# Weight folding ahead of the first norm, with its copies on ScalarE, and small matrices built on GpSimd, in a four-layer attention and gate kernel

## Chip, cores and metric

The kernel runs on one core of a Trainium2 chip. The time is the device time of one execution in microseconds (us); lower is better. The chip's engines are named as in the profile: PE is TensorE (matmuls), PEld its weight loads, DVE is VectorE, ACT is ScalarE, POOL is GpSimd, SP is SyncE. DVE and ACT can read PSUM in this kernel; POOL is only given tiles in SBUF.

## What is computed

The input is x, 16 samples of 256 channels by 32 x 32 positions, float32. Four layers follow one another:

```python
# layer 0: group norm, one-head attention over the 1024 positions, projection, residual
xn = group_norm(x); q, k, v = W_qkv xn + b
out = W_proj (softmax(q^T k / sqrt(C)) v) + b_proj + x
# layer 1: a gate from the channel mean and maximum
w3 = relu(conv3x3(concat[mean, max], w1)); gate = sigmoid(conv3x3(mean + max + w3, w2)); x = x * gate
# layer 2: group norm, attention, projection, residual, as layer 0 with other weights
# layer 3: attention with 32 query channels, logits clipped to +-10, scaled by gamma, residual
```

## The kernel before

**Layout.** A sample is held as channels on partitions (`x`, two chunks of 128 channels by 1024 positions) and once more by tokens (`xr`). Matrix products of two by two blocks are done with seven block products and a number of additions (`seven`, `weighted`), which is why tiles such as `xs`, `mc`, `vc`, `tc`, `tv` hold sums or differences of blocks. Logits and their exponentials are tiles `e` of 128 x 8 x 512.

**Folding (`fold`, from L301).** For layers 0 and 2 the weights are folded once, at the start of the program, and used for all samples. `transposed(j)` turns the query, key and value weights (`raw` -> PSUM `wtp` -> `wt`) with four TensorE transposes each, and two copies out of PSUM at L316. `multiplied` forms m = Wq^T Wk / 16 and wvp = Wv^T Wp with eight matmuls each (L322), and copies each half out of PSUM at L329. `right_sums` (L283 on) makes the block differences, on DVE for m (tile `mc`) and on POOL for wvp (tile `vc`). Two folded biases follow: `tbp` -> `tb` (L344, L351) and `brp` -> `bcol` (L365, L372).

**The head (`head`, `group_norm`).** Before a sample can be worked on, its channels are normalised in place: per-channel statistics (L114, L117), a transposed exchange inside the group (L119 to L134), a power on POOL (L138), scale and offset (L141 to L144), and the two passes over the data: chunk 0 on DVE (L145), chunk 1 on ACT (L146), 1024 positions each in one instruction. The first matmul on data, `tb_l` at L571, reads m and the normalised sample 0.

**The order.** The code is written as Python generators that are stepped in turn, and the framework then orders each engine's queue when the program is built: earlier-traced work goes first, as far as it is expected to be ready. Each engine works through its queue strictly in order on the chip. `keep_in_program_order` holds an instruction behind the one traced before it on the same engine. Before the change, the first line that is stepped is `in_turn([head(0), fold("l0", ...)])`: one step of sample 0's norm, one step of the layer-0 fold, and so on. After that two streams of samples (even and odd) start, the second 30 steps behind the first, and beside them `later()` runs: `head(1)` in turn with the fold of layer 2, then `fold3` (the small matrices of layer 3: `w` scaled at L400, copied into `w3qk` on POOL at L410, then matmuls `bias` L417 and L426, `qb`/`bcol` L434 to L437, and `strips` L380), then `build_toep`, then `checks`.

**`build_toep` (L84).** Three 128 x 32 matrices for the 3x3 convolutions, each the sum of nine terms: 27 instructions at L95 (compare and multiply) and 24 additions at L98, then three copies at L101. They are first read by the gate's matmul (L169).

**`checks` (from L871).** Five small tests that the weights are fit for this path. Each begins with `whole` (L294): a 128 x 512 copy at L297 and a 128 x 128 subtraction at L298, whose result a DVE instruction squares or weighs (`sq` L796, `msq` L831); PE then sums it (`size` L801, `reach` L845), and the result is counted on POOL (`n_ok`).

Of the kernel before, what the change touches and what calls it, by code (L numbers as in the profile page):

```python
# [12 lines left out]
AF = mybir.ActivationFunctionType  # L13
ALU = mybir.AluOpType
AX = mybir.AxisListType

P = 128
C = 256
CC = C // P
HW = 1024  # L20
NT = HW // P
HALF = 512
NH = HW // HALF
# [15 lines left out]
L0_GAMMA, L0_BETA, L0_BQ, L0_BK, L0_BP = range(5)  # L39
# [17 lines left out]
class Const:  # L57
# [26 lines left out]
    def build_toep(self, tc, work, tidx):  # L84

        nc = tc.nc
        for k in range(3):
            for tap in range(9):
                w = self.sc[:, S_W1 + 9 * k + tap : S_W1 + 9 * k + tap + 1]
                if tap == 0:  # L90
                    one = self.toep[:, k, :]
                else:
                    one = work.tile([P, STRIP], FP, tag="tap", name=f"tap_{k}_{tap}")
                tc.keep_in_program_order(
                    nc.vector.tensor_scalar(one, tidx, float(tap), w, ALU.is_equal, ALU.mult)  # L95
                )
                if tap:
                    nc.vector.tensor_tensor(self.toep[:, k, :], self.toep[:, k, :], one, ALU.add)  # L98
            yield
        for g in range(1, NG):  # L100
            nc.vector.tensor_copy(self.toep[:, 2 + g], self.toep[:, 2])  # L101
        nc.vector.tensor_scalar(self.neg_b2, self.sc[:, S_B2 : S_B2 + 1], -1.0, None, ALU.mult)
        yield


def group_norm(nc, k, small, xt, out, gamma, beta, nm, keep=None):

    st = small.tile([P, CC, 2, 6], FP, tag="st", name=f"st_{nm}", bufs=2)  # L110
    mv = k.moments
    for c in range(CC):
        for h in range(NH):
            first = nc.vector.bn_stats(st[:, c, h, :], xt[:, c, h * TPH : (h + 1) * TPH])  # L114
            if keep is not None:
                keep(first)
        nc.vector.bn_aggr(mv[:, 2 * c : 2 * c + 2], st[:, c, :, :])  # L117
    row = small.tile([P, GROUP], FP, tag="row", name=f"row_{nm}", bufs=2)
    nc.vector.transpose(row, mv)  # L119
    yield  # L120
    rst = small.tile([P, 6], FP, tag="rst", name=f"rst_{nm}", bufs=2)
    nc.vector.bn_stats(rst, row)
    rmv = small.tile([P, 2], FP, tag="rmv", name=f"rmv_{nm}", bufs=2)
    nc.vector.bn_aggr(rmv, rst)
    wide = small.tile([P, 2, GROUP], FP, tag="wide", name=f"wide_{nm}", bufs=2)
    nc.vector.tensor_copy(wide, rmv.unsqueeze(2).to_broadcast([P, 2, GROUP]))
    both = small.tile([P, 2, GROUP], FP, tag="both", name=f"both_{nm}", bufs=2)
    nc.vector.transpose(
        both.rearrange("p i n -> p (i n)"), wide.rearrange("p i n -> p (i n)")
    )  # L130

    gm = both[:, 0, 0 : 2 * CC : 2]
    ve = small.tile([P, CC], FP, tag="ve", name=f"ve_{nm}")
    nc.vector.scalar_tensor_tensor(  # L134
        ve, both[:, 0, 1 : 2 * CC : 2], EPS, both[:, 1, 0 : 2 * CC : 2], ALU.add, ALU.add
    )
    rstd = small.tile([P, CC], FP, tag="rstd", name=f"rstd_{nm}")
    nc.gpsimd.tensor_tensor(rstd, ve, k.neg_half, ALU.pow)  # L138
    yield
    a = small.tile([P, CC], FP, tag="a", name=f"a_{nm}")  # L140
    nc.vector.tensor_tensor(a, rstd, k.vec[:, :, gamma], ALU.mult)  # L141
    bb = small.tile([P, CC], FP, tag="bb", name=f"bb_{nm}")
    nc.vector.tensor_tensor(bb, gm, a, ALU.mult)
    nc.vector.tensor_tensor(bb, k.vec[:, :, beta], bb, ALU.subtract)  # L144
    nc.vector.tensor_scalar(out[:, 0], xt[:, 0], a[:, 0:1], bb[:, 0:1], ALU.mult, ALU.add)  # L145
    nc.scalar.activation(  # L146
        out[:, 1], xt[:, 1], AF.Identity, bias=bb[:, 1:2], scale=a[:, 1:2]
    )
    yield


# [50 lines left out]
def fast_path(nc, tc, k, bad, x, w_l0, w_l2, w_l3, qk_bias, v_bias, tap_idx, out):  # L202
# [7 lines left out]
    with ExitStack() as ctx:  # L210
# [83 lines left out]
        def whole(w, nm):  # L294

            full = work.tile([P, CC, C], FP, tag="oc", name=f"full_{nm}", bufs=3)
            tc.keep_in_program_order(nc.vector.tensor_copy(full, w))  # L297
            nc.vector.tensor_tensor(full[:, 0, P:], w[:, 1, P:], w[:, 0, P:], ALU.subtract)  # L298
            return full

        def fold(nm, which, base):  # L301


            w = raw[nm]
            wt = expp.tile([P, 3, CC, C], FP, tag="e", name=f"wt_{nm}")

            def transposed(j):
                for o in range(CC):
                    ps = bank(f"wtp_{nm}_{j}_{o}")
                    for c in range(CC):  # L310
                        nc.tensor.transpose(
                            ps[:, c * P : (c + 1) * P],
                            w[:, c, j * C + o * P : j * C + (o + 1) * P],
                            k.ident,
                        )
                    nc.vector.tensor_copy(wt[:, j, o, :], ps[:, :C])  # L316

            def multiplied(dst, left, right, scale):
                for c in range(CC):
                    ps = bank(f"fold_{nm}_{c}")  # L320
                    for o in range(CC):
                        nc.tensor.matmul(  # L322
                            ps[:, :C],
                            left[:, o, c * P : (c + 1) * P],
                            right[:, o, :],
                            start=(o == 0),
                            stop=(o == CC - 1),
                        )
                    nc.vector.tensor_scalar(dst[:, c, :], ps[:, :C], scale, None, ALU.mult)  # L329

            transposed(0)
            yield
            transposed(1)
            yield

            m = wts.tile([P, CC, C], FP, name=f"m_{nm}")
            multiplied(m, wt[:, 0], wt[:, 1], C**-0.5)
            yield
            mc = right_sums(nc.vector, m, f"mc_{nm}")
            tb = wts.tile([P, CC], FP, name=f"tb_{nm}")  # L340
            ps = bank(f"tbp_{nm}")
            for c in range(CC):
                for o in range(CC):
                    nc.tensor.matmul(  # L344
                        ps[:, c : c + 1],
                        wt[:, 1, o, c * P : (c + 1) * P],
                        k.vec[:, o, base + 2 : base + 3],
                        start=(o == 0),
                        stop=(o == CC - 1),
                    )  # L350
            nc.vector.tensor_scalar(tb, ps[:, :CC], C**-0.5, None, ALU.mult)  # L351
            yield
            transposed(2)
            yield
            wvp = wts.tile([P, CC, C], FP, name=f"wvp_{nm}")
            wp = w[:, :, 3 * C : 4 * C]
            multiplied(wvp, wt[:, 2], wp, 1.0)
            yield
            vc = right_sums(nc.gpsimd, wvp, f"vc_{nm}")

            bcol = bcol0 if nm == "l0" else bcol2
            ps = bank(f"brp_{nm}")
            for c in range(CC):
                for o in range(CC):
                    nc.tensor.matmul(  # L365
                        ps[:, c : c + 1],
                        wp[:, o, c * P : (c + 1) * P],
                        vcol[:, which, o : o + 1],
                        start=(o == 0),
                        stop=(o == CC - 1),  # L370
                    )
            nc.vector.tensor_tensor(bcol, ps[:, :CC], k.vec[:, :, base + 4], ALU.add)  # L372
            folded[nm] = m, mc, wvp, vc, tb
            yield
# [555 lines left out]
        def attend(xt, y, weights, lane, nm, then):  # L930
# [39 lines left out]
                then(h, tt.rearrange("p h c n -> p h (c n)"))  # L970
            count(ri, nm)

        def head(b):

            fetch(b)
            xt = loaded.pop(b)
            by_chunk = xt.rearrange("p t c n -> p c t n")
            xr = tokens[b] = load_tokens(b)
            keep = tc.keep_in_program_order if b == 1 else None
            yield from group_norm(  # L980
                nc, k, small, by_chunk, by_chunk, L0_GAMMA, L0_GAMMA + 1, f"l0_{b}", keep
            )
            ready[b] = xt, xr

# [173 lines left out]
        def in_turn(gens):  # L1158

            gens = list(gens)  # L1160
            while gens:
                for g in list(gens):
                    if next(g, gens) is gens:
                        gens.remove(g)
                    else:
                        yield
# [17 lines left out]
                    yield  # L1184
            do_chores(first)

        for _ in in_turn([head(0), fold("l0", 0, L0_GAMMA)]):
            pass


# [10 lines left out]
        ps = bank("badp")  # L1201
# [317 lines left out]
```

## Time and profile before

| | us |
|---|---|
| time, median of 3 runs (lowest to highest) | 2702.78 (2701.82 to 2702.98) |
| span of the profiled execution (no separate time of it is given) | 2702.3 |
| PE busy in the span | 2658.2 (98%) |
| DVE busy | 2153.9 (80%) |
| ACT busy | 1327.9 (49%) |
| POOL busy | 45.4 (2%) |
| first matmul of any kind / first matmul on sample data (`tb_l`) | 4.53 / 23.40 |

The span is cut into the busy and idle time of each engine. A row of the timeline reads: start in us, duration in us, engine, line, operation, tile written <- tiles read, shape, how many were merged, and in brackets how long the engine sat idle before it and who ended the wait. Merged instructions overlap a little, so a row's duration is from the first start to the last end. A row of the windows gives, for a stretch of time, the busy time and instruction count of PE, PEld, DVE, ACT and POOL, then the granted TensorE clock (1.00 is full speed).

### The profile page before, as it was taken

The page shows a single profiled execution, that of the slowest core. Times are in us where ns is not written, and L with a number is a line of the kernel's source. Part 1 is how long each engine was busy: PE and PEld are TensorE (multiplying, and loading weights), DVE is VectorE, ACT ScalarE, POOL GpSimd, SP SyncE. Part 2 cuts the span into 40 slices and gives each one's busy share as a digit, 9 for nine tenths or more (in the row PEclk, how much of TensorE's full clock was granted, in tenths as well). Part 3 has the DMA queues.
Part 4 walks back from the last instruction along what each step waited for, and adds up shares of the span by engine and source line. Part 5 has one row for each costly group of instructions (what it writes and reads, how often), then busy time and mean ns, then how long its engine had stood idle before and what let it go on. Part 6 is the DMA issues. An engine that isn't in the chain of part 4 may idle for free.

```text
span 2702.3 us, 47717 instructions
## 1 busy us (share of the span) xinstructions
PE 2658.2 (98%) x18998; PEld 2366.0 (88%) x18998; DVE 2153.9 (80%) x4242; ACT 1327.9 (49%) x2810; POOL 45.4 (2%) x118
## 2 busy tenths in 40 slices
PE   8999999999999999999999999999999999999997
PEld 6888988888988889889889898988989889898897
DVE  7988886888778887788867888678887788868776
ACT  3454455544455445544455544554454544545443
POOL 1000000000000000000000000000000000000000
PEclk9999999999999999999999999999999999999999
DMA  4021111212111120211201212112111121101111
GB/s 115 1 63 48 56 32 24 63 48 63 25 46 50 42 76 9 55 48 48 63 16 48 63 35 61 32 32 63 48 48 32 32 63 55 40 17 34 52 34 41
DMA packets 134823, 123.07 MB, mean 46 GB/s; under 512 B 10689, under 2 KB 125633, under 8 KB 134593
## 3 DMA queue, kind: packets, MB, share of 16 engines
q1 hardware_dynamic: 132720, 118.63, 15.7%
q8 instruction: 152, 2.49, 0.4%
q10 hardware_dynamic: 1872, 1.31, 0.2%
q14 instruction: 79, 0.64, 0.1%
HBM read 69.58 MB, written 50.33 MB: 44 GB/s over the span
## 4 chain that ended last, share of the span: by engine, by line
PE 81%; DVE 13%; ACT 4%; issue 2%; DMA 1%; POOL 0%; DVEq 0%; SPq 0%; ACTq 0%
PE b_l L571 15%; PE c_l L571 11%; PE af_l L571 11%; PE sb_l L571 10%; PE sc_l L571 8%; PE sf_l L571 4%; PE sa_l L571 3%; PE vb_l L571 3%; PE tb_l L571 3%; PE vc_l L571 2%; PE tc_l L571 2%; PE s L1107 2%; DVE e_l L603 1%; DVE vt L603 1%; PE vf_l L571 1%
## 5 line engine op out<-in xcount | busy, mean ns | idle before, releaser
L672 ACT COPY e_l<-sb_l 128x512 f32<-128x512 f32 x384 | 222.5, 584 | 217.9 <-PE sb_l L571 216.7
L571 PE MATMUL sb_l<-t_l,x 128*128 128x256 f32 x1024 | 262.0, 386 | 0.3
L571 PE MATMUL b_l<-vt,e_l 128*128 128x128 f32 x2048 | 251.8, 275 | 0.0
L571 PEld LDWEIGHTS b_l<-vt,e_l 128*128 128x128 f32 x2048 | 244.2, 192 | 5.4 <-issue 2.3
L571 PEld LDWEIGHTS sb_l<-t_l,x 128*128 128x128 f32 x1024 | 180.5, 191 | 40.1 <-ACT e_l L672 11.2
L682 ACT ACTIVATE e_l<-e_l 128x512 f32<-128x512 f32 x256 | 160.9, 630 | 86.6 <-DVE e_l L603 85.7
L684 ACT ACTIVATE e_l<-e_l 128x1024 f32<-128x1024 f32 x128 | 135.5, 1059 | 118.4 <-DVE e_l L603 118.4
L571 PE MATMUL c_l<-tv,cb_l 128*128 128x129 f32 x1536 | 189.0, 275 | 0.2 <-DVE cb_l L698 0.2
L571 PEld LDWEIGHTS c_l<-tv,cb_l 128*128 128x128 f32 x1536 | 180.3, 191 | 6.9 <-PE qk L1072 3.1
L603 DVE TENSOR_TENSOR e_l<-sc_l,e_l 128x512 f32<-128x512 f32 x128 | 88.0, 687 | 116.6 <-PE sc_l L571 114.9
L925 ACT COPY vt<-vb_l 128x512 f32<-128x512 f32 x144 | 84.5, 587 | 147.2 <-PE vb_l L571 146.1
L487 ACT ACTIVATE xr<-xr,bstrip 128x128 f32<-128x128 f32 (+1 forms) x376 | 134.4, 443 | 44.1 <-DVE xr L494 44.1
L1123 ACT ACTIVATE e<-s 128x512 f32<-128x512 f32 x256 | 131.8, 606 | 22.1 <-PE s L1107 21.4
L756 ACT COPY acc_l<-c_l 128x256 f32<-128x256 f32 x96 | 35.4, 368 | 212.3 <-DVE ri_l L755 151.8
L571 PE MATMUL sc_l<-tc_l,xs_l 128*128 128x256 f32 x512 | 134.0, 384 | 2.3 <-DVE vt L603 2.3
L571 PE MATMUL af_l<-tv,e_l 128*128 128x128 f32 x1024 | 131.6, 278 | 4.3 <-ACT e_l L682 4.3
L571 PE MATMUL sc_l<-t_l,xs_l 128*128 128x256 f32 x512 | 133.0, 382 | 0.8
L571 PE MATMUL sa_l<-t_l,x 128*128 128x256 f32 x512 | 132.4, 381 | 0.0
L571 PE MATMUL sf_l<-tc_l,x 128*128 128x256 f32 x512 | 131.7, 380 | 0.0
L571 PE MATMUL sb_l<-tc_l,xs_l 128*128 128x256 f32 x512 | 131.7, 379 | 0.0
L571 PEld LDWEIGHTS af_l<-tv,e_l 128*128 128x128 f32 x1024 | 121.3, 192 | 10.8 <-ACT e_l L682 7.7
L1128 DVE TENSOR_SCALAR e<-e 128x1024 f32<-128x1024 f32 x128 | 83.0, 687 | 59.0 <-ACT e L1123 59.0
(245 smaller groups left out, 5984.6 us busy)
## 6 DMA issues: line engine op xcount, KB each, us to landing
x<-mid_x SPq DMA_DIRECT2D x64, 512.0 KB, 3.3
xr<-in_x_dram SPq DMA_DIRECT2D x64, 256.0 KB, 4.9
mid_x<-t_z SPq DMA_DIRECT2D x128, 128.0 KB, 2.3
mid_x<-t_l SPq DMA_DIRECT2D x128, 128.0 KB, 2.3
x<-in_x_dram SPq DMA_DIRECT2D x62, 256.0 KB, 4.0
out_dram<-xr SPq DMA_DIRECT2D x124, 128.0 KB, 2.3
raw_l<-in_w_l_dram SPq DMA_DIRECT2D x1, 1024.0 KB, 6.9
raw_l<-in_w_l_dram SPq DMA_DIRECT2D x2, 256.0 KB, 5.5
```

The lines of the kernel that those rows point to most:

```text
L487: nc.scalar.activation(y[:, s, ts], y[:, s, ts], AF.Identity, bias=bias[:, s : s + 1])
L571: mm = nc.tensor.matmul(out, left, right, start=fresh and m == 0 and (lone or i == 0), stop=(m == len(pairs) - 1), skip_group_check=True,)
L603: nc.vector.tensor_tensor(dst, src, dst, ALU.add)
L672: nc.scalar.copy(block(i, j), ps.rearrange("p (m n) -> p m n", m=2))
L682: nc.scalar.activation(part, part, AF.Exp)
L684: nc.scalar.activation(e[:, m : m + 2, :], e[:, m : m + 2, :], AF.Exp)
L756: nc.scalar.copy(acc[:, hi, c2], c[:, :, :P])
L925: nc.scalar.copy(block(i, j), ps.rearrange("p (m n) -> p m n", m=TPH))
L1107: nc.tensor.matmul(ss[g][:, j * 2 * P : (j + 1) * 2 * P].rearrange("p (t g j) -> p t g j", t=TPH, g=2), qk[gs, mh, 1 - blk, j * P : (j + 1 ...
L1123: nc.scalar.activation(by_strip[:, :, :, qa], ss[g].rearrange("p (m t n) -> p m t n", m=2, t=TPH), AF.Exp,)
L1128: nc.vector.tensor_scalar(part, part, EXP_MIN, EXP_MAX, ALU.max, ALU.min)
```

## The change

The copies of the folds out of PSUM (L316, L329, L351) move from DVE to ACT. The first norm is stepped once (loads, statistics, first exchange), then the whole layer-0 fold is traced, then the rest of the norm. In that norm alone both data passes are cut in two halves of 512 positions, and its ACT halves are held behind the last ACT copy of the fold's transposes. `build_toep` and `whole` move from DVE to POOL. `group_norm`'s later uses keep one part. Nothing is computed otherwise.

```diff
 build_toep:
-                    nc.vector.tensor_scalar(one, tidx, float(tap), w, ALU.is_equal, ALU.mult)
+                    nc.gpsimd.tensor_scalar(one, tidx, float(tap), w, ALU.is_equal, ALU.mult)
-                    nc.vector.tensor_tensor(self.toep[:, k, :], self.toep[:, k, :], one, ALU.add)
+                    nc.gpsimd.tensor_tensor(self.toep[:, k, :], self.toep[:, k, :], one, ALU.add)
-            nc.vector.tensor_copy(self.toep[:, 2 + g], self.toep[:, 2])
+            nc.gpsimd.tensor_copy(self.toep[:, 2 + g], self.toep[:, 2])
 group_norm(..., keep=None, parts=1, behind=None):
-    nc.vector.tensor_scalar(out[:, 0], xt[:, 0], a[:, 0:1], bb[:, 0:1], ALU.mult, ALU.add)
-    nc.scalar.activation(
-        out[:, 1], xt[:, 1], AF.Identity, bias=bb[:, 1:2], scale=a[:, 1:2]
-    )
+    for i in range(parts):
+        ts = slice(i * NT // parts, (i + 1) * NT // parts)
+        nc.vector.tensor_scalar(
+            out[:, 0, ts], xt[:, 0, ts], a[:, 0:1], bb[:, 0:1], ALU.mult, ALU.add
+        )
+        other = nc.scalar.activation(
+            out[:, 1, ts], xt[:, 1, ts], AF.Identity, bias=bb[:, 1:2], scale=a[:, 1:2]
+        )
+        if behind is not None:
+            behind(other)
 whole:
-            tc.keep_in_program_order(nc.vector.tensor_copy(full, w))
-            nc.vector.tensor_tensor(full[:, 0, P:], w[:, 1, P:], w[:, 0, P:], ALU.subtract)
+            tc.keep_in_program_order(nc.gpsimd.tensor_copy(full, w))
+            nc.gpsimd.tensor_tensor(full[:, 0, P:], w[:, 1, P:], w[:, 0, P:], ALU.subtract)
 fold:
-                    nc.vector.tensor_copy(wt[:, j, o, :], ps[:, :C])
+                    copied.append(nc.scalar.copy(wt[:, j, o, :], ps[:, :C]))
-                    nc.vector.tensor_scalar(dst[:, c, :], ps[:, :C], scale, None, ALU.mult)
+                    nc.scalar.activation(dst[:, c, :], ps[:, :C], AF.Copy, scale=scale)
-            nc.vector.tensor_scalar(tb, ps[:, :CC], C**-0.5, None, ALU.mult)
+            nc.scalar.activation(tb, ps[:, :CC], AF.Copy, scale=C**-0.5)
+        def behind_folds(ins):
+            tc.add_manual_dep(ins.ins, copied[-1].ins.name, <order only, no wait>)
 head(b): group_norm(...)
-                nc, k, small, by_chunk, by_chunk, L0_GAMMA, L0_GAMMA + 1, f"l0_{b}", keep
+                nc, k, small, by_chunk, by_chunk, L0_GAMMA, L0_GAMMA + 1, f"l0_{b}", keep,
+                1 if b else NH,
+                None if b else behind_folds,
-        for _ in in_turn([head(0), fold("l0", 0, L0_GAMMA)]):
+        first_head = head(0)
+        next(first_head)
+        for _ in fold("l0", 0, L0_GAMMA):
+            pass
+        for _ in first_head:
             pass
```

## The prediction, made before the changed kernel was run

> **What bounds the kernel now.** The page first, for who is busy:
>
> ```profile
> PE 2658.2 (98%) x18998; PEld 2366.0 (88%) x18998; DVE 2153.9 (80%) x4242; ACT 1327.9 (49%) x2810; POOL 45.4 (2%) x118
> PE 81%; DVE 13%; ACT 4%; issue 2%; DMA 1%; POOL 0%; DVEq 0%; SPq 0%; ACTq 0%
> ```
>
> PE bounds it. The change removes no matmul, so it can win only where PE idles (2702.3 - 2658.2 = 44.1 us in all) or runs below full speed. About 15.3 us of the idle time lie in the last 102 us (86.73 busy in the stretch 2600 to 2702), which this change doesn't touch. So I read PE's own waits, between 20 and 80 us, then the timeline of the start, then the clock by windows.
>
> ```profile
> PE strips_l L380 <- DVE bcol L437: 0.8, 1, 0.8
> PE bias L417 <- POOL w3qk L410: 0.7, 1, 0.7
> PE fold_l L322 <- DVE wt_l L316: 0.6, 2, 0.3
> PE c_l L571 <- DVE cb_l L698: 0.2, 1, 0.2
> ```
>
> That is all that PE waits in 60 us: 2.3 us. Before 20 us it is more:
>
> ```profile
> 4.53 1.94 PE L311 MATMUL wtp_l<-ident,raw_l 128*128 128x128 f32 x8 [4.53 <-DMA raw_l<-in_w_l_dram]
> 13.30 3.78 PE L322 MATMUL fold_l<-wt_l 128*128 128x256 f32 x8 [6.83 <-DVE wt_l L316]
> 16.88 1.71 PE L344 MATMUL tbp_l<-vec,wt_l 128*128 128x1 f32 x8
> 18.45 1.09 PE L311 MATMUL wtp_l<-ident,raw_l 128*128 128x128 f32 x4
> 19.78 2.97 PE L322 MATMUL fold_l<-raw_l,wt_l 128*128 128x256 f32 x8 [0.23 <-DVE wt_l L316]
> 22.59 0.95 PE L365 MATMUL brp_l<-vcol,raw_l 128*128 128x1 f32 x8
> 23.40 1.10 PE L571 MATMUL tb_l<-x,m_l 128*128 128x512 f32 x2
> ...
> 40.90 1.99 PE L322 MATMUL fold_l<-raw_l,wt_l 128*128 128x256 f32 x8 [0.34 <-DVE wt_l L316]
> ```
>
> The transposes end at 6.47 and PE sits 6.83 us until DVE has copied them, because DVE does the norm's statistics first (its four copies start at 11.97, 12.38, 12.87 and 13.24). The eight fold matmuls take 3.78 us at 13.30 and the same eight 1.99 us at 40.90: PE starts at half speed. Weight loads took 0.333 us in the `tbp` group up to 18.2 and 0.19 in `brp` from 22.4, so full speed came near 22. (The windows write 1.00 for this part; the durations decide.) One more slow stretch is in the windows:
>
> ```profile
> 52.00:53.00 1.00, 0.16 (x3) 0.10 (x3) 0.90 (x6) 0.00 (x0) 0.20 (x1) 0.76 0.00 0
> 53.00:54.00 1.00, 1.00 (x9) 0.90 (x10) 0.80 (x4) 0.00 (x0) 0.92 (x3) 0.50 0.08 16
> ...
> 58.00:59.00 1.00, 1.00 (x4) 0.81 (x3) 1.00 (x8) 0.06 (x1) 0.00 (x0) 0.50 0.00 0
> 59.00:60.00 1.00, 1.00 (x5) 0.83 (x5) 0.66 (x4) 1.00 (x2) 0.00 (x0) 0.83 0.00 0
> ```
>
> The seventh column is the granted clock: half for some 6.8 us (52.5 to 59.3, worked out from the means 0.76 and 0.83 at its ends), which costs 3.4 us of work while PE looks busy. It follows 3.5 us (49.92 to 53.42) in which PE had only one-column and two-column matmuls (`bias`, `strips`) and the two waits of 0.7 and 0.8.
>
> **The change, part by part.** *Copies to ACT, fold 0 first.* ACT's last early DMA issue ends at 3.19 (2.56 + 0.63), and it computes nothing but a table load (1.28 us) before 14.74. A 128x256 copy from PSUM on ACT takes 0.37 us (`acc_l` L756, 0.368). If the table load lies before the transposes are done, the last of four copies ends at 6.5 + 0.4 = 6.9; if it begins only with the first finished bank (5.2), the third copy, enough to start, ends at 5.2 + 1.28 + 3 x 0.37 = 7.6. I take 7.2: the fold starts 6.1 us earlier (5.7 to 6.4). The chain from there to `tb_l` took 23.40 - 13.30 = 10.1 us and gets no more work, so `tb_l` could start at 17.3. The value weights for the second transposes came with issues at 2.56 and 2.83 and 5.5 us to landing, before 9: no wait.
>
> Is the sample ready by 17.3? Statistics end as before near 11.4; without four copies in between (in the chain of waits 0.31 + 0.33 + 0.32 us of them, the last merged with others) `a` and `bb` come some 0.6 us before 14.70, at 14.1. DVE's two halves (0.81 in all, say 0.43 each) end at 15.0. ACT's halves (0.69 each by `t_l` L947, same 512 columns) stand behind the copies of the second transposes: 7.2 + 3.78 + 1.5 + 1.1 + 0.6 = 14.2, so they end at 15.6. The block sum (0.69) ends at 16.3. All is hidden by the fold with 1.0 us to spare; without that cover, PE would wait up to 1 us. Nothing moves on SP: the four token loads of sample 0 lie in the first norm step, as before. POOL gets no DMAs.
>
> *The clock takes part of it back.* Full speed came some 8.7 us after the fold began (22.0 against 13.3). If it comes as long after the new beginning, all 6.1 us stay. If it comes at the same absolute time, PE does from 15.9 to 22.0 at half speed what it could do in half that: 6.1 - 3.05 = 3.05 us stay. Nothing here says which; I take the middle, **-4.6** (-6.1 to -3.0).
>
> The Trainium skill ("TensorE: Matmul & The Clock Gate", Part 1: The HAM clock gate) says that the clock is released after about 3.4 us of sustained work, judged in free-running windows. The trace took longer, 8.7 us, with the one-column `tbp` group in the middle. By the page alone full speed would come near 11, and the gain would be some 7.5 us.
>
> *Layer-2 fold and fold3.* `wvp` of layer 2 left PE at 42.9 but DVE copied it at 47.48, after 4.6 us of other work; POOL's `vc` (1.8 us) and `w3qk` (0.76 us) follow, and PE waits for them 0.65 us. On ACT, idle for 2.03 us before 46.42, the copies end near 44. The 0.65 us wait goes; the 0.8 us for `strips` may stay, since it is a DVE chain behind `bias`. With `bias` among logits rather than after them, the thin stretch falls below 3 us, and I take the half-clock stretch as gone: **-4.05** (0.65 + 3.4). Bounds: 0 if the stretch only moves, -4.9 if `strips` is covered too.
>
> *DVE relieved.* PE's wait of 0.34 at 40.90 goes: **-0.3** (0 to -0.8 with the 0.23 and 0.2). DVE loses 12 x 0.417 + 8 x 0.42 + 2 x 0.16 us of copies, 27 x 0.236 + 24 x 0.184 + 3 x 0.176 us of `toep`, 5 x (0.424 + 0.288) of `whole`, together 23.6 us of rows. But PE waits for DVE next to nothing there, so this itself is worth no more.
>
> *Costs.* ACT gets 12 x 0.37 + 8 x 0.42 (`junk`, 128x256, is 0.42) + 2 small, about 8.2 us; it was busy 16 of the 40 us from 20 to 60. Behind a copy of the layer-2 fold stand ACT's `t_l` and `vt` copies, and PE's next products wait for those (weight loads stood 0.75 us for `t_l` at 29.69). Four meetings of 0.37 us: **+1.5** (0 to 3).
>
> *POOL.* 54 `toep` instructions of 32 columns: nearest rows are 0.235 us (`w3qk` COPY, 128x64) and 0.457 us (`vc`, 128x128, two inputs), so 10 us at the least (54 x 0.19, the pace of the four copies) and 25 at the most; I take 0.27, nearer the smaller tile, 15 us. First reader is the gate (L169) at 132.5 us, over 55 us later: costs nothing. `full` for the first check stands behind it on POOL; `sq` on DVE waits for that, and `size` on PE for `sq`. Five `whole` are 5 x (0.5 to 1.8 + 0.46). DVE and POOL slow each other: `vc` L290 took 0.90 beside DVE's L905, which took 0.94 instead of 0.69; over 15 us that is at most some 15 x 0.25 us on a DVE relieved of more. I take 0.
>
> The skill ("GPSIMD Engine Reference", 4.1 Engine selection) advises against this: two-input elementwise work belongs on VectorE, which is about twice as fast. Here 128x128 took 0.457 on POOL and 0.287 on DVE, 1.6 times. Twice DVE's rows would make `toep` 22 us instead of 15, still ahead of 132.5 but not of the first check.
>
> **Sum:** -4.6 - 4.05 - 0.3 + 1.5 = -7.45 us on the span, 2702.3 -> 2694.85. The span lies 0.5 us (0.02%) under the median, so on the median: **2695.3**. A difference under 0.2%, 5.4 us, can't be told from none.
>
> **Rivals.**
> 1. *The slow stretch stays or moves.* `strips` still waits for DVE, and thin matmuls still follow each other; the trace shows one such drop after 3.5 thin us, and the new stretch is not much shorter. Then -4.6 - 0.3 + 1.5 = -3.4: 2699.4, within 0.2%.
> 2. *POOL becomes the wait (slower).* If DVE's queue has `sq` at about 61 us (where `size` stood on PE) while POOL, starting `toep` near 50, needs 25 us and 2 more for `full`, DVE stands until 77, 16 us, and PE behind it: 2695.3 + 16 = 2711. It ends slower than before by 0.2% from about 13 us of standing. For it: strict order of queues, `whole` pinned behind `toep`. Against: at 0.27 us the chain ends near 67, and checks begin with `whole` only after it; PE has other banks.
> 3. *The start doesn't move*: ACT's table load or a hidden wait holds the copies until the norm, or PE waits as long for sample 0. Then only -0.3 to -4: about 2700.5.
>
> **Chances.** The forecast 0.55 (2691 to 2697.4); better than that, full clock early and both waits gone (down to 2702.8 - 6.1 - 4.9 - 0.8 = 2691.0, or less with new overlap) 0.08; rival 1 0.19; rival 2 0.13; rival 3 0.05. Faster by over 0.2%: 0.63; within: 0.24; slower: 0.13. The range, 2689.5 to 2703.0, holds all but rival 2 and a little of the rest.
>
> **What would show it.** Right: `fold_l` at 7.2 and `tb_l` near 17.5; no 0.50 clock between 45 and 65; `vc_l` of layer 2 on POOL near 44; 0.2 to 0.3 us a `toep` instruction. Wrong: `tb_l` after 20, PE waiting for `x` L146; DVE idle before `sq` for POOL `full`; a half-clock stretch elsewhere.

## The result, and the profile after

| | before | changed |
|---|---|---|
| median (lowest to highest), 5 runs each | 2702.78 us (2700.66 to 2703.83) | 2713.41 us (2711.61 to 2715.26) |
| span of the profiled execution | 2702.3 us | 2711.5 us |

The changed kernel is slower: ratio 1.0037, 95% interval 1.0026 to 1.0049. The forecast was 2695.3 with a range to 2703.0, so the time lies outside the range and on the other side. Two things happened that partly cancel in the total, and the profile shows both. A few executions in which the clock stayed low (one of six in the first experiment below, 2737.77 us) are left out of every median and ratio.

First PE's timeline at the start of the changed kernel (the line numbers have moved: L311 is now L319, L322 is L330, L571 is L579):

```profile
4.95 1.94 PE L319 MATMUL wtp_l<-ident,raw_l 128*128 128x128 f32 x8 [4.95 <-DMA raw_l<-in_w_l_dram]
6.93 3.18 PE L330 MATMUL fold_l<-wt_l 128*128 128x256 f32 x8
10.25 1.05 PE L352 MATMUL tbp_l<-vec,wt_l 128*128 128x1 f32 x8
...
12.04 1.99 PE L330 MATMUL fold_l<-raw_l,wt_l 128*128 128x256 f32 x8 [0.24 <-ACT wt_l L324]
...
14.76 1.13 PE L579 MATMUL tb_l<-x,m_l 128*128 128x512 f32 x2
```

The fold follows the transposes at once, and the first product on sample data starts at 14.76 instead of 23.40: 8.6 us earlier. So the part meant to gain does gain, and more than forecast.

Then PE's waits in the whole changed kernel, longest first (in all, number, longest):

```profile
PE size_l L809 <- DVE sq_l L804: 17.1, 1, 17.1
...
PE fold_l L330 <- ACT wt_l L324: 2.6, 2, 2.4
```

One wait of 17.1 us, on the first of the five checks. The timeline around it, all engines, with most of POOL's and ACT's rows left out:

```profile
48.30 0.41 POOL L95 TENSOR_SCALAR toep<-tidx,sc 128x32 f32<-128x32 f32 x1
...
50.34 0.68 DVE L611 TENSOR_TENSOR e_l<-sa_l,e_l 128x512 f32<-128x512 f32 x1
...
52.30 1.13 PE L579 MATMUL sc_l<-t_l,xs_l 128*128 128x256 f32 x4
...
68.08 0.50 POOL L101 COPY toep<-toep 128x32 f32<-128x32 f32 x3
68.52 0.62 POOL L303 COPY full_v_l<-wvp_l 128x512 f32<-128x512 f32 x1
69.22 0.45 POOL L304 TENSOR_TENSOR full_v_l<-wvp_l 128x128 f32<-128x128 f32 x1
69.70 0.69 DVE L804 TENSOR_TENSOR sq_l<-full_v_l 128x512 f32<-128x512 f32 x1 [18.68 <-POOL full_v_l L304]
70.31 0.68 DVE L611 TENSOR_TENSOR e_l<-sc_l,e_l 128x512 f32<-128x512 f32 x1
...
70.54 1.19 PE L809 MATMUL size_l<-sq_l,ones 128*128 128x256 f32 x2 [17.11 <-DVE sq_l L804]
71.03 0.63 ACT L690 ACTIVATE e_l<-e_l 128x512 f32<-128x512 f32 x1 [16.58 <-DVE e_l L611]
```

Read from the bottom: ACT waits for a DVE addition, that addition stands in DVE's queue behind `sq`, `sq` waits for `full` from POOL, and `full` stands in POOL's queue behind 54 `toep` instructions that run from 48.30 to 68.58. PE's `size` waits for `sq`. Three engines stand for a check of the weights. The windows (PE, PEld, DVE, ACT, POOL busy, then the granted clock) show the same and its echo:

```profile
50.00:55.00 5.00, 3.43 (x16) 2.50 (x14) 1.02 (x2) 4.45 (x10) 4.09 (x14) 1.00 0.01 3
55.00:60.00 5.00, 0.00 (x0) 0.00 (x0) 0.00 (x0) 0.00 (x0) 4.17 (x14) 0.72 0.00 0
60.00:65.00 5.00, 0.00 (x0) 0.00 (x0) 0.00 (x0) 0.00 (x0) 4.25 (x14) 0.50 0.00 0
65.00:70.00 5.00, 0.00 (x0) 0.00 (x0) 0.30 (x1) 0.00 (x0) 3.95 (x13) 0.50 0.00 0
70.00:75.00 5.00, 4.46 (x16) 3.77 (x17) 1.67 (x4) 2.02 (x4) 0.00 (x0) 0.58 0.00 0
```

For about 15 us POOL is the only engine at work. The clock is halved from 57.2 to 74.2 (from the means 0.72 and 0.58), so after the wait PE does 3.7 us at half speed, 1.9 us lost.

The account on the spans: -8.6 (start) - 4.9 (the two waits at `fold3` and the slow stretch of before, all gone) + 4.8 (layer-2 copies on ACT, below) + 17.1 (wait) + 1.9 (half clock after it) = +10.3 us, against 9.2 measured. The remaining 1.1 us isn't accounted for.

### The profile page after: what moved, and what is told of

Its sections match the earlier page's. It is cut to its first block, busy times and chain, and to the rows that moved or that the text cites. A ratio compares the mean times of both kernels' runs of the same rounds, so it can differ in the third digit from the quotient of the medians.

```text
span 2711.5 us, 47725 instructions
## 1 busy us (share of the span) xinstructions
PE 2655.9 (98%) x18998; PEld 2363.5 (87%) x18998; DVE 2140.1 (79%) x4157; ACT 1334.3 (49%) x2833; POOL 68.9 (3%) x182
## 3 DMA queue, kind: packets, MB, share of 16 engines
q1 hardware_dynamic: 132720, 118.63, 15.9%
## 4 chain that ended last, share of the span: by engine, by line
PE 79%; DVE 14%; ACT 4%; issue 2%; POOL 1%; DMA 0%; DVEq 0%; SPq 0%; ACTq 0%
PE b_l L579 15%; PE af_l L579 11%; PE c_l L579 11%; PE sb_l L579 10%; PE sc_l L579 8%; PE sf_l L579 4%; PE sa_l L579 3%; PE vb_l L579 3%; PE tb_l L579 2%; PE vc_l L579 2%; PE s L1136 2%; PE tc_l L579 1%; DVE e_l L611 1%; DVE vt L611 1%; PE qk L1101 1%
## 5 line engine op out<-in xcount | busy, mean ns | idle before, releaser
L579 PE MATMUL sb_l<-t_l,x 128*128 128x256 f32 x1024 | 262.9, 387 | 0.3
L579 PE MATMUL b_l<-vt,e_l 128*128 128x128 f32 x2048 | 252.0, 275 | 0.0
L579 PEld LDWEIGHTS b_l<-vt,e_l 128*128 128x128 f32 x2048 | 244.4, 192 | 5.6 <-issue 2.3
L579 PEld LDWEIGHTS sb_l<-t_l,x 128*128 128x128 f32 x1024 | 181.2, 191 | 40.2 <-ACT e_l L680 11.0
L579 PE MATMUL c_l<-tv,cb_l 128*128 128x129 f32 x1536 | 188.9, 275 | 0.0
L579 PEld LDWEIGHTS c_l<-tv,cb_l 128*128 128x128 f32 x1536 | 180.3, 191 | 6.5 <-PE qk L1101 3.1
L495 ACT ACTIVATE xr<-xr,bstrip 128x128 f32<-128x128 f32 (+1 forms) x376 | 134.0, 440 | 43.9 <-DVE xr L502 43.9
L579 PE MATMUL af_l<-tv,e_l 128*128 128x128 f32 x1024 | 131.5, 278 | 4.3 <-ACT e_l L690 4.3
L579 PE MATMUL sc_l<-tc_l,xs_l 128*128 128x256 f32 x512 | 133.1, 382 | 2.3 <-DVE vt L611 2.3
L579 PE MATMUL sc_l<-t_l,xs_l 128*128 128x256 f32 x512 | 133.2, 382 | 0.9 <-ACT e_l L680 0.2
L579 PE MATMUL sb_l<-tc_l,xs_l 128*128 128x256 f32 x512 | 131.5, 379 | 0.0
L579 PE MATMUL sa_l<-t_l,x 128*128 128x256 f32 x512 | 131.5, 379 | 0.0
L579 PE MATMUL sf_l<-tc_l,x 128*128 128x256 f32 x512 | 131.4, 379 | 0.0
L579 PEld LDWEIGHTS af_l<-tv,e_l 128*128 128x128 f32 x1024 | 121.2, 192 | 10.8 <-ACT e_l L690 7.7
L579 PE MATMUL b_l<-vt,e 128*128 128x128 f32 x1024 | 126.1, 276 | 4.2 <-DVE e L1157 4.2
```

Source lines behind the costliest of these rows:

```text
L495: nc.scalar.activation(y[:, s, ts], y[:, s, ts], AF.Identity, bias=bias[:, s : s + 1])
L579: mm = nc.tensor.matmul(out, left, right, start=fresh and m == 0 and (lone or i == 0), stop=(m == len(pairs) - 1), skip_group_check=True,)
```

## The experiments

The theory after reading this: POOL's queue order costs the time, and the folds' part is a gain (T). The rivals: the copies on ACT or the early norm cost it (R1); POOL and DVE slow each other while `toep` runs (R2). Medians are of 4 to 12 executions, and a ratio is to runs of the kernel before on the same chip (2703 to 2704 us there, about 1 us more than above; so a difference of two medians from different chips is good to some 1 us).

**Check copies back on DVE, `toep` still on POOL.**

```diff
-            tc.keep_in_program_order(nc.gpsimd.tensor_copy(full, w))
-            nc.gpsimd.tensor_tensor(full[:, 0, P:], w[:, 1, P:], w[:, 0, P:], ALU.subtract)
+            tc.keep_in_program_order(nc.vector.tensor_copy(full, w))
+            nc.vector.tensor_tensor(full[:, 0, P:], w[:, 1, P:], w[:, 0, P:], ALU.subtract)
```

> The changed kernel with the check copies (whole) back on DVE; toep stays on POOL. Theory T (the first check's full stands on POOL behind some 20 us of toep, DVE's sq waits for it 18.7 us and PE's size 17.1 us, and PE then starts at half clock): both waits go, worth 17.1 + some 1.9 us, so 2713.4 - 19 = 2694, and the size row has no wait over 1 us. Rival R1 (the copies on ACT or the early norm cost the time): it stays above 2702. Rival R2 (POOL and DVE slow each other while toep runs): the toep rows are the same, so it is slower than the folds alone by several us.

2694.59 us, ratio 0.9966 (0.9954 to 0.9979). No wait on `size` is left; the clock stays at 1.00 from 40 to 140 us:

```profile
40.00:60.00 20.00, 19.50 (x128) 17.34 (x127) 12.94 (x31) 13.38 (x27) 13.83 (x37) 1.00 0.01 2
60.00:80.00 20.00, 20.00 (x115) 17.02 (x114) 18.87 (x42) 10.51 (x25) 10.94 (x28) 1.00 0.00 1
```

POOL is as busy as ever (13.83 and 10.94 us of 20) and PE full. Ten instructions on another engine are worth 18.8 us.

**`build_toep` back on DVE, check copies on POOL.**

```diff
-                    nc.gpsimd.tensor_scalar(one, tidx, float(tap), w, ALU.is_equal, ALU.mult)
+                    nc.vector.tensor_scalar(one, tidx, float(tap), w, ALU.is_equal, ALU.mult)
...
-                    nc.gpsimd.tensor_tensor(self.toep[:, k, :], self.toep[:, k, :], one, ALU.add)
+                    nc.vector.tensor_tensor(self.toep[:, k, :], self.toep[:, k, :], one, ALU.add)
...
-            nc.gpsimd.tensor_copy(self.toep[:, 2 + g], self.toep[:, 2])
+            nc.vector.tensor_copy(self.toep[:, 2 + g], self.toep[:, 2])
```

> The changed kernel with build_toep back on DVE; the check copies stay on POOL. T: full follows the layer-3 sums on POOL at once (near 49 us), so sq waits little: 2694, within 2 us of the run with the check copies on DVE. If it is the POOL place of the check copies itself that costs: still above 2705. R1: above 2702.

2693.84 us, ratio 0.9963 (0.9950 to 0.9976), the fastest kernel of the study, though it can't be told from the run above or the next. It is faster than the kernel before and than the changed one. So neither move hurts alone: the pair does, because one stands in front of the other in one queue.

**Folds only:** both diffs above together.

> Only the folds' copies on ACT, the fold ahead of the norm and the norm in two parts; toep and check copies on DVE. T: tb_l at 14.8 instead of 23.4 stays worth 8.6 us, less a 2.4 us wait for the layer-2 copies on ACT: 2692 to 2696. R1: 2703 or more. R2: several us faster than the run that only takes the check copies back.

2695.08 us, ratio 0.9966 (0.9953 to 0.9979). R1 falls: copies, order and split norm together gain 8.8 us. R2 falls too: with `toep` on POOL the time was 2694.59, the same. So is the time with the check copies alone on POOL (2693.84): the moves to POOL gain nothing even where they do no harm.

**POOL part alone, on the kernel before:** both diffs above reversed, applied to the old kernel.

> The kernel before with toep and check copies on POOL and nothing else changed. T: toep starts near 54.7 (after the layer-3 sums) and takes 20 us, full ends near 76, PE stands from about 60 for 15 us and restarts at half clock: 2702.8 + 15 to 19 = 2718 to 2722. R1: no more than 2705, since the folds are as before. R2: some 3 us slower without a long PE wait.

2720.26 us, ratio 1.0060 (1.0048 to 1.0073): 16.4 us slower, with the folds untouched. PE has one long wait behind the start, in the same place:

```profile
PE size_l L801 <- DVE sq_l L796: 16.9, 1, 16.9
```

The two parts add up roughly, -8.8 + 16.4 = 7.6 us against 10.6 for both. The profile of this run shows where a good part of the 3 us can be. Its start is the code of the kernel before, and yet `tb_l` began at 22.20 instead of 23.40:

```profile
13.57 3.78 PE L322 MATMUL fold_l<-wt_l 128*128 128x256 f32 x8 [7.16 <-DVE ve_l L134]
19.56 1.99 PE L322 MATMUL fold_l<-raw_l,wt_l 128*128 128x256 f32 x8 [0.69 <-DVE wt_l L316]
22.20 1.10 PE L571 MATMUL tb_l<-x,m_l 128*128 128x512 f32 x2
```

The second fold ran at full speed here (1.99 us against 2.97), and the half-clock stretch at `fold3` lasted 3.4 us instead of 6.8. That is 1.2 + 1.7 = 2.9 us which the same code won by where its half-clock stretches fell; the one after its long wait cost 1.0 us more than in the changed kernel (5.8 us of work at half speed instead of 3.7).

**Checks stepped before `build_toep`**, everything on POOL as in the change.

```diff
-            yield from k.build_toep(tc, work, tidx)
             yield from checks()
+            yield from k.build_toep(tc, work, tidx)
```

> The changed kernel, all its POOL work kept, but checks are stepped before build_toep. T (order on POOL is what costs, not POOL's pace): the first full follows the layer-3 sums near 49 us, sq and size don't wait, toep runs in POOL's gaps and is done long before the gate near 125: 2693 to 2696. If POOL's pace costs in itself: above 2705, with waits for later check copies.

2698.79 us, ratio 0.9983 (0.9974 to 0.9992). Order alone takes 14.6 of the 18.8 us back. My number was 3 us too low: now `toep` is late for its own reader,

```profile
PE c_l L188 <- POOL toep L101: 1.8, 1, 1.8
```

the gate's second product at 132.7 us, whose cover I had put at 55 us. With `checks` first, `toep` stands on POOL behind the count of the last check (`n_ok` at 107.84) and runs from 108.0 to 132.7: 24.7 us, where the changed kernel took 20.3 with DVE standing still. Beside DVE's long additions four of its instructions took 1.00 to 1.45 us instead of 0.25 to 0.40:

```profile
128.46 1.45 POOL L95 TENSOR_SCALAR tap<-tidx,sc 128x32 f32<-128x32 f32 x1
128.50 1.23 DVE L754 TENSOR_TENSOR e_l<-cb_l,e_l 128x1024 f32<-128x1024 f32 x1
```

So R2's mechanism is real for POOL, and here it is what makes `toep` late. PE also waits 1.3 us for ACT's exponentials, and near 38 us it has 3.4 us at half clock (1.7 us lost) that the run with the check copies on DVE happens not to have; the three come to 4.8 us, of 4.2 between the medians and 6.7 between the two profiles.

**The size of a POOL instruction:** the weight in L95 replaced by the constant 0.1, so the convolutions' weights are left out.

```diff
-                    nc.gpsimd.tensor_scalar(one, tidx, float(tap), w, ALU.is_equal, ALU.mult)
+                    nc.gpsimd.tensor_scalar(one, tidx, float(tap), 0.1, ALU.is_equal, ALU.mult)
```

> The changed kernel with the convolution weight replaced by the constant 0.1 in build_toep's 27 compare-and-multiply instructions (the convolutions' weights are left out). Measures what makes them 0.396 us against 0.250 us for the additions. If it is the per-partition scalar read: they fall to about 0.25, the chain shortens by 27 x 0.15 = 4 us and so does PE's wait, 13 instead of 17 us, 2709. If it is the two operations or the kind of instruction: 0.39 us and 17 us as they were, 2713.

The changed kernel first, then this run:

```profile
L95 POOL TENSOR_SCALAR tap<-tidx,sc 128x32 f32<-128x32 f32 x24 | 9.5, 396 | 1.2
...
L95 POOL TENSOR_SCALAR tap<-tidx 128x32 f32<-128x32 f32 x24 | 7.7, 320 | 1.6
L98 POOL TENSOR_TENSOR toep<-toep,tap 128x32 f32<-128x32 f32 x24 | 6.0, 250 | 2.0
```

Between the two guesses: 0.396 fell to 0.320, not to 0.25. The chain fell from 20.3 to 19.0 us and PE's wait from 17.1 to 15.9 us; the median from 2713.41 to 2712.40, which the spread doesn't resolve. The per-partition scalar costs 0.076 us here; what makes the other 0.07 stays open.

**Which queue stands: `size` later in PE's queue** (16 steps instead of 4 between `sq` and `size`), then the same **with `sq` on POOL too** (the line in brackets).

```diff
 alike:
-                nc.vector.tensor_tensor(sq.rearrange("p (c o) -> p c o", c=CC), w, w, ALU.mult)
+                [nc.gpsimd.tensor_tensor(sq.rearrange("p (c o) -> p c o", c=CC), w, w, ALU.mult)]
-            yield from pause()
+            yield from wait(16)
```

> The changed kernel with 16 instead of 4 steps between sq and size in alike, so that PE's queue has size some 20 places later, while DVE's sq stays where it was. Tells which of the two queues makes the stall. If DVE's place decides (T): DVE still stands some 18 us before sq, PE runs dry waiting for DVE's additions (L611) instead of size, 2709 to 2714. If PE's place decides: PE no longer waits over 3 us, 2694 to 2697.

> As the last, and sq (a 128x512 product) on POOL too, so that nothing on DVE stands behind POOL's toep; POOL still does all its work in the same order. T (DVE's strict queue behind POOL is the cost): no long wait on DVE or PE, 2693 to 2698. If POOL's load slows the others by itself: above 2703.

With `size` later, 2716.80 us (ratio 1.0045, 1.0030 to 1.0061), some 3 us above the range I gave T. The wait has only changed its name, since DVE still stands behind `sq` (PE's waits first):

```profile
PE af_l L579 <- ACT e_l L690: 17.4, 1, 17.4
```

and in DVE's own waits

```profile
DVE sq_l L804 <- POOL full_v_l L304: 19.9, 2, 18.8
```

DVE's place decides, not PE's. With `sq` on POOL as well both long waits are gone, but the time is 2706.32 us (ratio 1.0010, 1.0000 to 1.0019), 8 us above the range I expected from T. ACT now has

```profile
ACT junk L1029 <- POOL sq_l L804: 6.1, 1, 6.1
```

`junk`, `full` and `sq` share three buffers, so ACT's mean of sample 0 waits until POOL has let one go; PE waits 4.3 us behind it. The slow chain was still on the path, through a buffer instead of a queue. The profile is 11.2 us longer than that of the run with the check copies on DVE. Besides the 4.3 us it has three half-clock stretches of 3.4 us that the other lacks between 12 and 81 us, some 1.5 us each; one follows this wait, the other two have nothing to do with POOL (near 14 and 38 us). The rest isn't divided further.

**`toep` early on POOL**, stepped in turn with `head(1)` and the layer-2 fold.

```diff
+            tiles = k.build_toep(tc, work, tidx)
-            yield from in_turn([head(1), fold("l2", 1, L2_GAMMA)])
+            yield from in_turn([tiles, head(1), fold("l2", 1, L2_GAMMA)])
...
-            yield from k.build_toep(tc, work, tidx)
             yield from checks()
```

> The changed kernel with build_toep stepped early, in turn with head(1) and the layer-2 fold, so that POOL builds the matrices from about 19 us on, in its idle time, and full follows the layer-3 sums directly. T: no wait at sq or size; but POOL is strict in order here too, and rstd of sample 1 and vc of layer 2 now stand behind toep, by up to 5 us against 27.9 and 37.3. If DVE and PE have other work there: 2693 to 2696, as good as toep on DVE. If the wait only moves to DVE's a (L141): 2698 to 2702.

2702.14 us, ratio 0.9990 (0.9982 to 0.9999): the worse case of the two. The power of sample 1's norm now stands behind `toep`, DVE behind it, PE behind DVE. DVE's waits, then PE's:

```profile
DVE a_l L141 <- POOL rstd_l L138: 8.7, 1, 8.7
```

```profile
PE sf_l L579 <- DVE vt L611: 6.0, 1, 6.0
```

DVE stood 8.7 us where I had expected up to 5. And the wait costs about as much again behind it: the clock is 0.50 from 35.2 to 48.9, so PE does the 9.9 us after its wait at half speed, 4.9 us lost.

**The gaining part, taken apart.** Copies on ACT without the new order, on the kernel before:

```diff
-                    nc.vector.tensor_copy(wt[:, j, o, :], ps[:, :C])
+                    nc.scalar.copy(wt[:, j, o, :], ps[:, :C])
-                    nc.vector.tensor_scalar(dst[:, c, :], ps[:, :C], scale, None, ALU.mult)
+                    nc.scalar.activation(dst[:, c, :], ps[:, :C], AF.Copy, scale=scale)
-            nc.vector.tensor_scalar(tb, ps[:, :CC], C**-0.5, None, ALU.mult)
+            nc.scalar.activation(tb, ps[:, :CC], AF.Copy, scale=C**-0.5)
```

> The kernel before with only the folds' copies on ACT: fold and norm still stepped in turn, norm in one part, nothing on POOL. T: the copies are what frees PE at 6.5 us, so fold_l starts near 7 and tb_l near 15 to 17: 2694 to 2697. Rival (the order of the steps is needed too): ACT's norm pass gets in front of the fold's copies, tb_l after 18, above 2698.

2701.15 us, ratio 0.9994 (0.9985 to 1.0003): the rival holds, the order is needed too. The fold starts at 6.50, but then:

```profile
10.53 0.64 PE L311 MATMUL wtp_l<-ident,raw_l 128*128 128x128 f32 x4
15.56 3.61 PE L322 MATMUL fold_l<-raw_l,wt_l 128*128 128x256 f32 x8 [4.39 <-ACT wt_l L316]
```

ACT's copies of the value weights wait behind the norm pass on the same engine; `tb_l` starts at 19.81.

The other half: the folds-only kernel with this diff reversed, and `None` in place of `behind_folds`, so that the order and the norm in two parts are all that is left.

> Only the order: the layer-0 fold stepped wholly before the rest of the first norm, the norm in two parts; copies, toep and check copies all on DVE as before. Expected: DVE still does the statistics until 10.8 us first, so the copies move by 1 to 2 us at most and fold_l starts at 11 to 12.5 instead of 13.3: 2700 to 2702. If the order alone does it: tb_l below 17 and 2697 or less.

2703.18 us, ratio 1.0000 (0.9991 to 1.0010), as DVE still does the statistics first (`fold_l` at 13.85, later than I expected, after a wait of 7.37 us). Neither half is told from nothing by its median; both together are 8.8 us.

**Layer-2 value copies on DVE**, check copies on DVE as well.

```diff
-                    copied.append(nc.scalar.copy(wt[:, j, o, :], ps[:, :C]))
+                    if nm == "l2" and j == 2:
+                        nc.vector.tensor_copy(wt[:, j, o, :], ps[:, :C])
+                    else:
+                        copied.append(nc.scalar.copy(wt[:, j, o, :], ps[:, :C]))
```

> Check copies back on DVE as in the first run, and the layer-2 fold's last two weight copies (wt, value weights) on DVE too, so that they don't stand behind ACT's eight token additions (L495). T: PE's 2.4 us wait for ACT wt goes: 2694.8 - 2.4 = 2692. If DVE is no better there (it is busy too): 2694 to 2695.

2694.79 us (0.9958 to 0.9980), no gain: in its profile PE waits 0.8 us for DVE at that fold instead of 2.4 us for ACT, but the profiled execution was the slowest of the seven (2698.54 us) and had a half-clock stretch over the second fold (`tb_l` at 16.64), so what the edit is worth by itself stays open.

## Why the prediction was wrong, step by step

**The start of the fold** was right: 6.93 against 7.2. The sample was ready in time: ACT's and DVE's halves began at 14.16, and PE never waited for `x`, though without the 1.0 us to spare, because PE came 2.5 us earlier than I had worked out. The block sum ended at 17.04 instead of 16.3, and PE waited 0.4 us for `bcol`, which stood behind it.

**The clock term was mis-sized**: -4.6 us taken, -8.6 measured for `tb_l`. The durations show why. `tbp` took 1.05 us instead of 1.71, the second fold 1.99 instead of 2.97: full speed came near 9.4, some 2.4 us after the fold began, where I assumed at least 8.7. Those 8.7 us, and with them the 10.1 us from the fold to `tb_l`, were one execution's and not the kernel's. Two other runs whose fold began as late (POOL part alone, 13.57; only the order, 13.85) came to `tb_l` in 8.6 and 8.1 us. So of the 8.6 us gained between the two profiles, 6.4 are the earlier fold, and most of the other 2.2 is a profile of before that ran longer at half clock than others do.

The Trainium skill ("TensorE: Matmul & The Clock Gate", Part 1: The HAM clock gate), read alone, gave full speed near 11 and 7.5 us of gain, nearer than my middle. The 7.5 isn't worked out there; halving the stretch from 11 to 15.9, as the prediction does elsewhere, gives an estimate of 6.1 + 2.45 = 8.5 us.

**The slow stretch at `fold3`** went, as forecast: clock 1.00 from 45 to 55, `vc` of layer 2 on POOL at 37.27, earlier than the 44 I wrote. A shorter one came elsewhere, which the prediction had named as a sign of being wrong. **The cost of ACT's load was mis-sized**: 1.5 us taken, about 4.8 found, and in the other direction: I priced ACT's other copies behind those of the fold, but the layer-2 value copies stood behind eight token additions (`xr` L495, 3.29 us) in ACT's queue:

```profile
35.64 2.82 PE L330 MATMUL fold_l<-raw_l,wt_l 128*128 128x256 f32 x8 [2.39 <-ACT wt_l L324]
```

That is 2.4 us of waiting, 0.7 us for `vt` before it, and a half-clock stretch of 3.4 us after it (2.82 us instead of 1.99 for the fold), which costs 1.7 us in all. The last part is chance: three other profiles with the same wait have no such stretch (below).

**The step that failed is POOL's, priced at 0.** The pace was in its bounds: L95 0.396 us and L98 0.250 us against 0.27, the chain 20.3 us long against 15 (10 to 25). What was wrong is the sentence that let it cost nothing: that the checks begin with `whole` only after the chain, and that PE has other banks. By the prediction's own numbers the chain ended near 67, after the 61 it gave `sq`, so DVE would have stood some 6 us. Queue order isn't made by who is done when: DVE's `sq` stood right after the additions of 50.3 us and PE's `size` behind the product of 52.3, eighteen microseconds ahead of POOL. Other work for PE doesn't help: with `size` moved back in its queue PE stood 17.4 us all the same, for exponentials whose additions stand behind `sq`. Rival 2 names this mechanism (16 us, 2711; it was 18.7 us on DVE, 17.1 on PE, 2713.4). I gave it 0.13. That its size came so near is luck: it put `sq` at 61 us and the end of the chain at 77, and they were at 51 and 69.7, both too late by 7 to 10 us. The trace of before had a hint that I read past, in the waits of the kernel before:

```profile
DVE a_l L141 <- POOL rstd_l L138: 18.8, 24, 0.8
```

In 24 of 32 norms DVE stood for the whole POOL instruction (0.69 us): the order left this reader of POOL no slack. For a chain of 54 POOL instructions ahead of another DVE reader, its full length was the first price to take, not zero.

The rule of the Trainium skill against this move ("GPSIMD Engine Reference", 4.1 Engine selection) held as a direction: `full`'s copy took 0.61 us on POOL against 0.42 on DVE, the subtraction 0.45 against 0.29. POOL's pace sets how long the wait is (with the constant weight, 1.3 us off the chain took 1.2 us off the wait), but the order decides whether there is one: with `toep` or the check copies alone in POOL's queue the same instructions cost nothing.

## What to carry to other kernels

Moving work to an idle engine is free only if nobody with a strict queue waits for what comes after it there: before the move, list the first reader of each moved result and of everything queued behind it, and price the whole chain at that reader's place in its own queue. Ask too what the move can win: PE didn't wait for `toep` or the check copies while they were on DVE, so moving them won nothing. And measure such a change in its parts: here a gain of 8.8 us and a loss of 16.4 us came as one.

## What the runs showed of the hardware

- TensorE's half-clock stretch outlasts the idle time that causes it: after 17.1 us of waiting the clock stayed at 0.50 for another 3.7 us of dense work, and after a wait of 6.0 us (`toep` early on POOL) for another 9.9 us. In the kernel before, 3.5 us of one- and two-column matmuls with 1.5 us of waits were followed by a halved clock of 6.8 us; the same instructions in the run with the POOL part alone were followed by 3.4 us of it.
- Whether such a stretch comes isn't fixed by the program alone. The wait of 2.4 us at the layer-2 fold was followed by 3.4 us at 0.50 in four profiles (the changed kernel, folds only, checks first, `size` later) and by none in three (check copies on DVE, `toep` on DVE, the constant weight). At the start, `tb_l` began between 14.28 and 14.96 us in the eight profiles whose second fold ran at full speed, and at 16.50 and 16.64 in two others of the same order, where the clock was 0.50 for 3.4 us over that fold (3.53 and 3.16 us instead of 1.99). In those two PE had just waited 1.0 and 1.4 us for a small load (`vec`), elsewhere 0.9 us or less; that this is the cause isn't shown. A term of a few us that is read from a single profile can be such chance.
- POOL and DVE slow each other (layer 0's `vc` L296 took 0.90 us beside DVE's `xs` L912, which took 0.94 instead of 0.69). Beside DVE's 128x1024 additions small POOL instructions took up to 1.45 us instead of 0.40 (checks first), while the additions themselves took 1.21 to 1.29 us, against 1.18 to 1.22 where POOL was idle (`size` later). The medians show no cost of this where nobody waits for POOL (2694.59 with `toep` on POOL, 2695.08 without).
